# A message-passing layer: vector operations over messages cut to 128 columns and spread over the units

## The chip, the cores and the metric

The kernel runs on one core of a Trainium2 chip. The core has a matrix engine (TensorE, PE in the profile; PEld is its weight load), a vector engine (VectorE, DVE), an engine for activations (ScalarE, ACT), GpSimd (POOL), which here issues the indirect gathers, and SyncE (SP), which issues the other DMAs. The metric is the device time of one execution in microseconds; the median of three runs counts.

## The reference

There are 6250 nodes with 256 features and 206250 edges, sorted by their target `dst`. Cut to what matters:

```python
h = relu(layernorm(x))
polarity = clip(edge_attr[:, 0:1], 0, 1)
e = relu(edge_attr[:, 1:] @ W_e1.T + b_e1) @ W_e2.T + b_e2      # 64 -> 256 -> 256
edge_emb = (e * (polarity + 0.01)) @ W_le.T + b_le
msg = relu(h[src] + edge_emb)
aggr = segment_sum(msg, dst, num_segments=6250)
g = layernorm((h + aggr) @ W_g1.T + b_g1) * ln_g + ln_b
out = x + relu(g) @ W_g2.T + b_g2
```

All of it is in float32.

## The kernel before, in words

The two products W_e2 and W_le are multiplied once into one matrix (`wc_s`), and the polarity is a number per edge, so that it can be multiplied in at the end. Edges lie in tiles of 128. A block is four tiles (512 edges), a unit is half a block (two tiles, 256 edges; there are 806 units, numbered `u`), a pair is two blocks, and a group is six blocks (24 tiles, 3072 edges; 68 groups). Nodes are worked on in 49 windows of 128.

First the statistics of the rows of x are made and h + b_le is written to a table in HBM (`hb_d`, L370, L372). Meanwhile the edge work of the first 22 units begins. The main loop (L710) then runs over the units. For each unit:

- `forward(u)` computes the edge part: eight matrix instructions on PE (L266; every listed matmul is two of them in the profile) fill one PSUM tile, and one DVE add (L271) takes it to `msg[u]` in SBUF. There are seven such PSUM tiles in rotation (`pz`); the first layer, the edge part and the node work all draw on them.
- Once every eight units (in the middle of the run, `by_two`), right behind one unit's edge part, `turn_of` runs the first layer of two pairs (L243, 16 matrix instructions that need eight PSUM tiles, six taken away by ACT at L251 and two by DVE at L248), then `add_pairs`, which sums finished messages into the groups with one-hot matrices (L566), and then loads the raw edge data ahead. I call the eight units from one such place to the next a round.
- `gathers(...)` puts the gathers of later units on the POOL queue (L528): two indirect DMAs per unit, 128 rows of the table each, into one of 16 buffers `hg`. The first gather of such a call also waits for the last matmul of the unit's edge part.
- `whole(made)` makes the message: per tile one DVE operation hg = msg x polarity + hg over 256 columns (L551), both large operands and the output in SBUF, the polarity a column of one number per partition; then one RELU on ACT for the unit (L556). It runs behind the edge part by `LEAD - u // 36` units, 22 at first and 1 at last, so that messages and gathers go a little faster than units.
- `due()` runs at most one step that has fallen due. The steps are the one-hot matrices of a later group (`select`, L541: one DVE comparison over 24 x 32 = 768 columns) and the node work of a window: `spread` loads x, its transpose `hT` and the row statistics `stb` and makes the window's one-hot matrices (L629); `ready(0)` and `ready(1)` (L639) multiply and add the statistics to `hT` over 256 columns; `offset` (L205) adds a bias to x; `rows_of`, `one`, `two` and `three` are the matrix steps.

The order on each engine is the order of the calls (a manual schedule): DVE works its list strictly in that order, and so does POOL. So what stands behind a waiting instruction on DVE waits with it. The calls in the loop, cut:

```python
for u in range(LEAD, NU):
    now = u
    forward(u)
    ...
        gathers(4 * summed + HG - 8 + (1, 2, 3, 4, 5, 6, 6, 7)[k], last_z)
    ...
    while made < u + 1 - max(LEAST, LEAD - u // SHRINK) - (by_two(u // 4) and (u + 1) % 8 == TURN):
        whole(made)
        made += 1
    due()
```

Of the kernel before, what the change touches and what calls it, by code (L numbers as in the profile page):

```python
# [51 lines left out]
def group_of(b):  # L52
    return b // L


def blocks_of(g):
    return range(g * L, min((g + 1) * L, NB))
# [36 lines left out]
def gnn_kernel(ctx: ExitStack, tc: tile.TileContext, x, src_c, dst_c, dst_r, pol_c, raw_t, w_e1t, w_e2,  # L94
# [16 lines left out]

    ident = const.tile([P, P], F32, name="ident")
    eps_t = const.tile([P, 1], F32, name="eps_t")
    we1_s = const.tile([P, D], F32, name="we1_s")
    wc_s = const.tile([P, 2, D], F32, name="wc_s")
    bc_s = const.tile([P, 2, D], F32, name="bc_s")
# [27 lines left out]
    def finish_nodes(nd, ps, w, n):  # L144

        r = w * P

        def turn(a):
            pt = ps()
            for c in range(2):  # L150
                nc.tensor.transpose(pt[:, 0, c * P:c * P + n], a[:n, c * P:(c + 1) * P], ident[:n, :n])
            aT = nd.tile([P, 2, P], F32, name="aT")
            if n == P:
                nc.scalar.activation(aT, pt[:, 0, :].rearrange("p (c n) -> p c n", c=2), AF.Copy)
            else:
                for c in range(2):
                    nc.scalar.activation(aT[:, c, :n], pt[:, 0, c * P:c * P + n], AF.Copy)
            return aT

        def first(aT, bias_by_pe=False):  # L160
            ph = ps()
            if bias_by_pe:
                nc.tensor.matmul(ph[:n, 0, :], ones[0:1, :n], bg1_b[0:1], start=True, stop=False)
            for c in range(2):
                nc.tensor.matmul(ph[:n, 0, :], aT[:, c, :n], wg1_s[:, c, :], start=c == 0 and not bias_by_pe, stop=c == 1)  # L165
            hs = nd.tile([P, D], F32, name="hs")
            if bias_by_pe:
                hb = ph[:, 0, :]
            else:
                hb = hs  # L170
                nc.vector.tensor_add(hs[:n], ph[:n, 0, :], bg1_b[:n])
            mv = row_stats(nd, n, 1, lambda i: hb[:n])
            rs = nd.tile([P, 1], F32, name="rs1")
            one_over_std(rs[:n], mv, n)
            nc.vector.tensor_scalar(hs[:n], hb[:n], mv[:n, 0, 0:1], rs[:n], op0=ALU.subtract, op1=ALU.mult)
            return hs

        def second(hs):
            pt = ps()
            for c in range(2):  # L180
                nc.tensor.transpose(pt[:, 0, c * P:c * P + n], hs[:n, c * P:(c + 1) * P], ident[:n, :n])  # L181
            nT = nd.tile([P, 2, P], F32, name="nT")
            for c in range(2):
                nc.scalar.activation(nT[:, c, :n], pt[:, 0, c * P:c * P + n], AF.Relu, bias=lnb_s[:, c:c + 1],  # L184
                                     scale=lng_s[:, c:c + 1])
            return nT

        def third(nT, xt):
            po = ps()
            for c in range(2):  # L190
                nc.tensor.matmul(po[:n, 0, :], nT[:, c, :n], wg2_s[:, c, :], start=c == 0, stop=c == 1)  # L191
            ot = nd.tile([P, D], F32, name="ot")
            nc.vector.tensor_add(ot[:n], po[:n, 0, :], xt[:n])
            for i, (a, b) in enumerate(spread_out(n)):
                eng = nc.scalar if i else nc.sync
                eng.dma_start(out=out[bass.ds(r + a, b - a), :], in_=ot[a:b])

        def load_x():
            xt = nd.tile([P, D], F32, name="xt3")
            for a, b in spread_out(n):  # L200
                nc.sync.dma_start(out=xt[a:b], in_=x[bass.ds(r + a, b - a), :])
            return xt

        def offset(xt):
            nc.vector.tensor_add(xt[:n], xt[:n], bg2_b[:n])  # L205

        return turn, first, second, third, load_x, offset

# [3 lines left out]
    with fast:  # L212
# [11 lines left out]
        def ps():  # L224
            return psz.tile([P, 2, D], F32, name="pz")
# [74 lines left out]
                turn_of(u // 4)  # L300

        nc.vector.memset(eps_t, EPS)
        nc.vector.memset(ones, 1.0)
        nc.vector.memset(rs_s, 0.0)
        nc.vector.memset(nm_s, 0.0)
# [207 lines left out]
        with tc.tile_pool(name="hg", bufs=HG) as hg_p, tc.tile_pool(name="ms", bufs=5) as ms_p, \  # L513
# [21 lines left out]

            def select(g):

                n = len(blocks_of(g)) * S
                t = g * L * S
                sel[g] = sel_p.tile([P, L * S, W], F32, name="sel")  # L540
                nc.vector.tensor_tensor(  # L541
                    sel[g][:, :n, :], iota_w.rearrange("p (o w) -> p o w", o=1).to_broadcast([P, n, W]),
                    rel[:, t:t + n].rearrange("p (t o) -> p t o", o=1).to_broadcast([P, n, W]), ALU.is_equal)

            def whole(u):

                m = msg.pop(u)
                if plain(u):
                    nc.vector.tensor_add(m, m, bc_s)
                for i in range(2):  # L550
                    nc.vector.scalar_tensor_tensor(hg[u][:, i, :], m[:, i, :], pol_s[:, 2 * u + i:2 * u + i + 1],  # L551
                                                   hg[u][:, i, :], op0=ALU.mult, op1=ALU.add)
                    if u == NU - 1:
                        nc.scalar.activation(hg[u][:, i, :], hg[u][:, i, :], AF.Relu)
                if u < NU - 1:
                    nc.scalar.activation(hg[u], hg[u], AF.Relu)  # L556

            def add_up(b):

                g = group_of(b)  # L560
                k = b - g * L
                if k == 0:
                    acc[g] = pd[:, g % 2, :] if g < NG - 1 else ps()[:, 0, :]
                for j in range(S):
                    m = hg[2 * b + j // 2]
                    nc.tensor.matmul(acc[g][j * W:(j + 1) * W, :], sel[g][:, k * S + j, :], m[:, j % 2, :],  # L566
                                     start=k == 0, stop=b == blocks_of(g)[-1])
                hg.pop(2 * b)
                hg.pop(2 * b + 1)
                return g if b == blocks_of(g)[-1] else None  # L570
# [16 lines left out]
            def add_pairs(last=False):  # L587

                nonlocal summed
                whole_groups = []  # L590
                while summed < NP and min(4 * summed + 4, NU) < made + last:
                    for b in (2 * summed, 2 * summed + 1):
                        if b < NB:
                            whole_groups.append(add_up(b))
                            if b % L == 0 and group_of(b) + 2 < NG:
                                at(now + 2, lambda g=group_of(b) + 2: select(g))
                    summed += 1

                for g in whole_groups:
                    keep(g)  # L600
# [2 lines left out]
            todo = {}  # L603
            now = 0
            late = {}
            ending = {-2: [], -1: []}

            def at(u, fn):
# [2 lines left out]
            def node_work(w, spread_now=False):  # L611
# [7 lines left out]
                def spread():  # L619
# [7 lines left out]
                    for g in gs:  # L627
# [1 line left out]
                        nc.vector.tensor_scalar(s2, iota_p, rowid[:, g:g + 1], float(-w * P), op0=ALU.subtract,  # L629
                                                op1=ALU.is_equal)  # L630
                        box["sel2"].append(s2)
                    at(now + 3, lambda: ready(0))
                    at(now + 4, lambda: ready(1))
                    at(now + 5, lambda: offset(box["xt"]))

                def ready(i):

                    hT, st = box["hT"], box["st"]
                    nc.vector.tensor_tensor(hT[:, :, :n], hT[:, :, :n], st[:, i:i + 1, :n].to_broadcast([P, 2, n]),  # L639
                                            (ALU.mult, ALU.add)[i])  # L640

                def sums_of(part):

# [56 lines left out]

            gathers(HG)
            sums = add_pairs
            for i, fn in ((0, first_rows), (1, rows_of_edges), (3, lambda: select(0)), (5, row_numbers), (6, stats_out),
                          (7, lambda: select(1)), (8, node_weights)):
                at(LEAD + i, fn)
            for i, fn in enumerate((by_group(0, ALU.max), by_group(1, ALU.min), by_row(0, ALU.max), by_row(1, ALU.min),
                                    verdict, count, total)):
# [2 lines left out]
            for u in range(LEAD, NU):  # L710
# [8 lines left out]
                else:  # L719
                    gathers(4 * summed + HG - 4 + (u - TURN) % 4 + 1, last_z)  # L720

                while made < u + 1 - max(LEAST, LEAD - u // SHRINK) - (by_two(u // 4) and (u + 1) % 8 == TURN):
                    whole(made)
                    made += 1
                due()
                if u == NU - 24:
                    for w in range(NW):
                        if groups_of(w)[-1] == NG - 1:
                            late[w] = node_work(w, True)
                if u == LEAD + 60:  # L730
                    flag = nc.values_load(bad_i[0:1, 0:1], min_val=0, max_val=3 * P)
            while todo:
                now = min(todo)
                for fn in todo.pop(now):
                    fn()
            before, last = ending[-2], ending[-1]
            for sums_of, halves_out, rows_of, one, two, three, gs in before:
                rows_of()
# [28 lines left out]
def any_order(tc, dram, v):  # L767
# [7 lines left out]
    with tc.tile_pool(name="sc", bufs=1) as sc, tc.tile_pool(name="sk", bufs=2) as sk, \  # L775
# [78 lines left out]
        def nodes(w, n):  # L854
# [1 line left out]
            nc.sync.dma_start(out=ac[:n], in_=acc_d[bass.ds(w * P, n), :])  # L856
            turn, one, two, three, load_x, offset = v["finish_nodes"](sk, lambda: sp1.tile([P, 1, D], F32, name="ps_a"), w, n)
            xt = load_x()
            offset(xt)
            three(two(one(turn(ac))), xt)  # L860

        with tc.For_i(0, full, 1) as w:
# [65 lines left out]
```

## Time and profile before

| what | value |
|---|---|
| median of the runs | 2187.48 us (2186.34 to 2188.13, three runs) |
| the profiled execution | 2189.23 us, its span 2187.4 us |
| mean granted TensorE clock | 0.997 |
| PE, PEld busy | 2169.5, 1625.1 us |
| DVE busy | 1604.4 us |
| ACT busy | 960.8 us |
| POOL busy | 1648.4 us |
| DMA | 309.17 MB, mean 141 GB/s |

A row of the page's table of groups names the line, the engine, the operation, what it writes and reads, its shape and count; then the busy time in us and the mean duration of one in ns; then the idle time of that engine just before such instructions, and what ended most of it. Busy times count overlapping instructions once, and an instruction may start before the one ahead of it on its engine has ended, so a mean duration is longer than the distance between two starts. In a list of waits the columns are the waiting group, what it waited for, the total in us, the number of times and the longest. A timeline line gives start and length in us; several instructions of one kind in a row are merged, with their number behind x.

### The profile page before, as it was taken

How to read it: one execution, taken by the hardware profiler on the slowest of the kernel's cores; microseconds unless marked ns; L12 is line 12 of the kernel's file. 1: busy time of each engine (PE TensorE's matmuls, PEld its weight loads, DVE VectorE, ACT ScalarE, POOL GpSimd, SP SyncE). 2: the span in 40 equal slices, each digit the busy share in tenths (PEclk: the TensorE clock that was granted, in tenths of full speed). 3: DMA queues.
4: the chain of work that ended last, by engine and by line, in shares of the span. 5: the costliest groups of instructions: out<-in, count | busy, mean ns of one | idle time of the engine just before them, and what ended most of it. 6: DMA issues, size and time to landing. Idle time of an engine off the chain costs nothing.

```text
span 2187.4 us, 34907 instructions
## 1 busy us (share of the span) xinstructions
PE 2169.5 (99%) x12382; PEld 1625.1 (74%) x12382; DVE 1604.4 (73%) x3470; ACT 960.8 (44%) x1701; POOL 1648.4 (75%) x1675
## 2 busy tenths in 40 slices
PE   9999999999999999999999999999999999999998
PEld 6677777777777777777677777777777777777776
DVE  7787777777777777777677777777777767777675
ACT  7444444444444444444444444343444444444443
POOL 5777777777777777777777777777777777777775
PEclk9999999999999999999999999999999999999999
DMA  9544445454545454545544445445444445454543
GB/s 313 159 134 134 138 126 157 130 149 122 151 126 155 119 155 125 151 123 151 142 122 139 142 139 151 129 121 156 139 131 128 143 130 153 131 146 130 150 123 89
DMA packets 156075, 309.17 MB, mean 141 GB/s; under 512 B 33183, under 2 KB 77944, under 8 KB 155896
## 3 DMA queue, kind: packets, MB, share of 16 engines
q0 software_dynamic: 77376, 211.39, 33.7%
q1 hardware_dynamic: 77364, 92.23, 13.7%
q10 hardware_dynamic: 1156, 3.28, 0.4%
q8 instruction: 98, 1.61, 0.3%
q14 instruction: 81, 0.66, 0.1%
HBM read 293.92 MB, written 12.85 MB: 140 GB/s over the span
## 4 chain that ended last, share of the span: by engine, by line
PE 92%; DMA 3%; POOL 2%; DVE 2%; issue 1%; ACT 1%; ACTq 0%; DVEq 0%; POOLq 0%
PE pz L266 60%; PE pz L243 16%; PE pd L566 9%; PE pz L664 3%; DMA hg<-hb_d,src_s 3%; PE pz L165 2%; PE pz L191 2%; POOL hg L528 2%; DVE msg L271 1%; PE pz L181 1%; DMA xt<-in_x_dram 0%; ACT xt L366 0%; DVE hg L551 0%; DVE st L136 0%; PE pz L307 0%
## 5 line engine op out<-in xcount | busy, mean ns | idle before, releaser
L528 POOL DMA_INDIRECT hg<-hb_d,src_s x1612 | 1611.2, 999 | 495.5 <-issue 355.3
L266 PE MATMUL pz<-wc_s,e 128*128 128x256 f32 x6448 | 1452.3, 381 | 1.3 <-ACT msg L269 1.3
L266 PEld LDWEIGHTS pz<-wc_s,e 128*128 128x128 f32 x6448 | 1208.7, 190 | 203.8 <-issue 28.8
L556 ACT ACTIVATE hg<-hg 128x512 f32<-128x512 f32 x805 | 500.5, 629 | 1048.0 <-DVE hg L551 1030.5
L551 DVE SCALAR_TENSOR_TENSOR hg<-msg,pol_s,hg 128x256 f32<-128x256 f32 x1612 | 711.3, 478 | 153.3 <-DMA hg<-hb_d,src_s 148.9
L271 DVE TENSOR_TENSOR msg<-pz,bc_s 128x512 f32<-128x512 f32 x799 | 542.9, 685 | 224.0 <-PE pz L266 223.0
L243 PE MATMUL pz<-raw,we_s 64*128 64x512 f32 x1612 | 402.8, 608 | 6.9 <-DVE msg L271 6.6
L251 ACT ACTIVATE e<-pz,vecs 128x512 f32<-128x512 f32 x605 | 361.8, 692 | 88.0 <-PE pz L243 86.9
L243 PEld LDWEIGHTS pz<-raw,we_s 64*128 64x128 f32 x1612 | 160.2, 186 | 195.6 <-issue 127.2
L248 DVE TENSOR_SCALAR e<-pz,vecs 128x512 f32<-128x512 f32 x201 | 150.5, 749 | 164.6 <-PE pz L243 164.6
L566 PE MATMUL pd<-hg,sel 128*32 128x256 f32 x3216 | 196.9, 386 | 0.0
L566 PEld LDWEIGHTS pd<-hg,sel 128*32 128x32 f32 x3216 | 95.0, 110 | 129.3 <-issue 77.6
L664 PEld LDWEIGHTS pz<-s,ms 128*128 128x128 f32 x548 | 68.7, 192 | 3.1 <-issue 0.4
L664 PE MATMUL pz<-s,ms 128*128 128x128 f32 x548 | 69.3, 275 | 0.1
L541 DVE TENSOR_TENSOR sel<-iota_w,rel 128x768 f32<-128x768 f32 x68 | 63.9, 940 | 0.0
L370 POOL TENSOR_TENSOR hb<-xt,rows_b 128x256 f32<-128x256 f32 (+1 forms) x49 | 34.1, 728 | 24.2 <-ACT xt L366 18.2
L191 PE MATMUL pz<-wg_s,nT 128*128 128x256 f32 (+1 forms) x196 | 50.6, 380 | 0.6 <-ACT nT L184 0.6
L165 PE MATMUL pz<-wg_s,hT 128*128 128x256 f32 (+1 forms) x196 | 50.5, 380 | 0.0
L577 ACT ACTIVATE ms<-pd 128x256 f32<-128x256 f32 x66 | 25.4, 384 | 51.5 <-PE pd L566 51.5
L191 PEld LDWEIGHTS pz<-wg_s,nT 128*128 128x128 f32 (+1 forms) x196 | 37.1, 190 | 5.9 <-ACT nT L184 0.8
L165 PEld LDWEIGHTS pz<-wg_s,hT 128*128 128x128 f32 (+1 forms) x196 | 37.0, 190 | 5.7 <-issue 0.3
L639 DVE TENSOR_TENSOR hT<-hT,stb 128x256 f32<-128x256 f32 x98 | 40.8, 417 | 0.0
(90 smaller groups left out, 378.2 us busy)
## 6 DMA issues: line engine op xcount, KB each, us to landing
raw<-in_raw_t_dram SPq DMA_DIRECT2D x202, 256.0 KB
hg<-hb_d,src_s POOLq DMA_INDIRECT x1612
stb<-st_d SPq DMA_DIRECT2D x49, 128.0 KB
hb_d<-hb SPq DMA_DIRECT2D x12, 512.0 KB
xt<-in_x_dram SPq DMA_DIRECT2D x48, 128.0 KB
hT<-in_x_t_dram SPq DMA_DIRECT2D x48, 128.0 KB
out_dram<-ot SPq DMA_DIRECT2D x48, 128.0 KB
xt<-in_x_dram SPq DMA_DIRECT2D x11, 512.0 KB
```

Of the source, the lines that this page charges most:

```text
L165: nc.tensor.matmul(ph[:n, 0, :], aT[:, c, :n], wg1_s[:, c, :], start=c == 0 and not bias_by_pe, stop=c == 1)
L191: nc.tensor.matmul(po[:n, 0, :], nT[:, c, :n], wg2_s[:, c, :], start=c == 0, stop=c == 1)
L243: nc.tensor.matmul(pe[s, c], we1_s[s * F:(s + 1) * F, c * P:(c + 1) * P], raw[q][s * F:(s + 1) * F, :], start=True, stop=True)
L248: nc.vector.tensor_scalar(e1[b][:, c, :], pe[s, c], be1_s[:, c:c + 1], 0.0, op0=ALU.add, op1=ALU.max)
L251: nc.scalar.activation(e1[b][:, c, :], pe[s, c], AF.Relu, bias=be1_s[:, c:c + 1])
L266: last_z = nc.tensor.matmul(pz[:, i, :], e1[b][:, c, k:k + P], wc_s[:, c, :], start=c == 0, stop=c == 1)
L271: nc.vector.tensor_add(msg[u], pz, bc_s)
L528: g = nc.gpsimd.indirect_dma_start(out=hg[u][:, i, :], out_offset=None, in_=hb_d, in_offset=bass.IndirectOffsetOnAxis(ap=src_s[:, 2 * u + ...
L551: nc.vector.scalar_tensor_tensor(hg[u][:, i, :], m[:, i, :], pol_s[:, 2 * u + i:2 * u + i + 1], hg[u][:, i, :], op0=ALU.mult, op1=ALU.add)
L556: nc.scalar.activation(hg[u], hg[u], AF.Relu)
L566: nc.tensor.matmul(acc[g][j * W:(j + 1) * W, :], sel[g][:, k * S + j, :], m[:, j % 2, :], start=k == 0, stop=b == blocks_of(g)[-1])
L664: nc.tensor.matmul(pa[:, c, :n], ms[g][:, c * P:(c + 1) * P], box["sel2"][i][:, :n], start=i == 0, stop=i == len(gs) - 1)
```

## The change

The products of `whole` become two operations of 128 columns each in place of one of 256. The one-hot of a group is no longer one comparison of 768 columns but six of 128, one per block; `ready` works on one half of `hT` at a time and `offset` on one half of x. These pieces also change their form: a two-operand TENSOR_TENSOR becomes a SCALAR_TENSOR_TENSOR that first adds a column of zeros (`zero_c`), so that the values stay the same. They leave the list of due steps and go into two queues, `steps` (h and x; due three units after the loads) and `rest` (one-hot). `piece()` runs one of them per unit, between the edge part's add and the products; where more than six one-hot pieces wait, a second runs after `due()`. The first sums of a group first run what is left of its one-hot.

```diff
+    zero_c = const.tile([P, 1], F32, name="zero_c")
...
-        def offset(xt):
-            nc.vector.tensor_add(xt[:n], xt[:n], bg2_b[:n])
+        def offset(xt, c):
+            h = slice(c * P, (c + 1) * P)
+            nc.vector.scalar_tensor_tensor(xt[:n, h], xt[:n, h], zero_c[:n], bg2_b[:n, h], op0=ALU.add, op1=ALU.add)
...
             def select(g):
-                n = len(blocks_of(g)) * S
-                t = g * L * S
-                sel[g] = sel_p.tile([P, L * S, W], F32, name="sel")
-                nc.vector.tensor_tensor(
-                    sel[g][:, :n, :], iota_w.rearrange("p (o w) -> p o w", o=1).to_broadcast([P, n, W]),
-                    rel[:, t:t + n].rearrange("p (t o) -> p t o", o=1).to_broadcast([P, n, W]), ALU.is_equal)
+                return [(g, lambda k=k: rows_of_block(g, k)) for k in range(len(blocks_of(g)))]
+
+            def rows_of_block(g, k):
+                t = (g * L + k) * S
+                if k == 0:
+                    sel[g] = sel_p.tile([P, L * S, W], F32, name="sel")
+                nc.vector.scalar_tensor_tensor(
+                    sel[g][:, k * S:(k + 1) * S, :], iota_w.rearrange("p (o w) -> p o w", o=1).to_broadcast([P, S, W]),
+                    zero_c, rel[:, t:t + S].rearrange("p (t o) -> p t o", o=1).to_broadcast([P, S, W]), op0=ALU.add,
+                    op1=ALU.is_equal)
+
+            def piece():
+                if steps and steps[0][0] <= now:
+                    steps.popleft()[1]()
+                elif rest:
+                    rest.popleft()[1]()
...
                 for i in range(2):
-                    nc.vector.scalar_tensor_tensor(hg[u][:, i, :], m[:, i, :], pol_s[:, 2 * u + i:2 * u + i + 1],
-                                                   hg[u][:, i, :], op0=ALU.mult, op1=ALU.add)
+                    for c in range(2):
+                        h = slice(c * P, (c + 1) * P)
+                        nc.vector.scalar_tensor_tensor(hg[u][:, i, h], m[:, i, h], pol_s[:, 2 * u + i:2 * u + i + 1],
+                                                       hg[u][:, i, h], op0=ALU.mult, op1=ALU.add)
...
                 if k == 0:
                     acc[g] = pd[:, g % 2, :] if g < NG - 1 else ps()[:, 0, :]
+                    while rest and rest[0][0] <= g:
+                        rest.popleft()[1]()
...
                             if b % L == 0 and group_of(b) + 2 < NG:
-                                at(now + 2, lambda g=group_of(b) + 2: select(g))
+                                rest.extend(select(group_of(b) + 2))
...
-                    at(now + 3, lambda: ready(0))
-                    at(now + 4, lambda: ready(1))
-                    at(now + 5, lambda: offset(box["xt"]))
+                    steps.extend((now + 3, lambda i=i, c=c: ready(i, c)) for i in range(2) for c in range(2))
+                    steps.extend((now + 3, lambda c=c: offset(box["xt"], c)) for c in range(2))
-                def ready(i):
+                def ready(i, c):
                     hT, st = box["hT"], box["st"]
-                    nc.vector.tensor_tensor(hT[:, :, :n], hT[:, :, :n], st[:, i:i + 1, :n].to_broadcast([P, 2, n]),
-                                            (ALU.mult, ALU.add)[i])
+                    nc.vector.scalar_tensor_tensor(hT[:, c, :n], hT[:, c, :n], zero_c, st[:, i, :n], op0=ALU.add,
+                                                   op1=(ALU.mult, ALU.add)[i])
...
-            for i, fn in (..., (3, lambda: select(0)), ..., (7, lambda: select(1)), (8, node_weights)):
+            for i, fn in (..., (3, lambda: rest.extend(select(0) + select(1))), ..., (8, node_weights)):
...
                 else:
                     gathers(4 * summed + HG - 4 + (u - TURN) % 4 + 1, last_z)
 
+                piece()
                 while made < ...:
                     whole(made)
                     made += 1
                 due()
+                if len(rest) > 6:
+                    piece()
...
+            while steps:
+                steps.popleft()[1]()
```

More of the change, by code (lines that the diff above doesn't have):

```diff
@@ L302, in gnn_kernel @@
         nc.vector.memset(eps_t, EPS)
+        nc.vector.memset(zero_c, 0.0)
         nc.vector.memset(ones, 1.0)
@@ L605, in gnn_kernel @@
             late = {}
+            steps = deque()
+            rest = deque()
             ending = {-2: [], -1: []}
@@ L702, in gnn_kernel @@
             sums = add_pairs
-            for i, fn in ((0, first_rows), (1, rows_of_edges), (3, lambda: select(0)), (5, row_numbers), (6, stats_out),
-                          (7, lambda: select(1)), (8, node_weights)):
+            for i, fn in ((0, first_rows), (1, rows_of_edges), (3, lambda: rest.extend(select(0) + select(1))), (5, row_numbers), (6, stats_out),
+                          (8, node_weights)):
                 at(LEAD + i, fn)
@@ L858, in nodes @@
             xt = load_x()
-            offset(xt)
+            offset(xt, 0)
+            offset(xt, 1)
             three(two(one(turn(ac))), xt)
```

## The prediction

> **What bounds the kernel now.** I read the page's first part and its groups first, for who is busy and with what.
>
> ```profile
> PE 2169.5 (99%) x12382; PEld 1625.1 (74%) x12382; DVE 1604.4 (73%) x3470; ACT 960.8 (44%) x1701; POOL 1648.4 (75%) x1675
> ...
> L528 POOL DMA_INDIRECT hg<-hb_d,src_s x1612 | 1611.2, 999 | 495.5 <-issue 355.3
> ...
> L551 DVE SCALAR_TENSOR_TENSOR hg<-msg,pol_s,hg 128x256 f32<-128x256 f32 x1612 | 711.3, 478 | 153.3 <-DMA hg<-hb_d,src_s 148.9
> L271 DVE TENSOR_TENSOR msg<-pz,bc_s 128x512 f32<-128x512 f32 x799 | 542.9, 685 | 224.0 <-PE pz L266 223.0
> L243 PE MATMUL pz<-raw,we_s 64*128 64x512 f32 x1612 | 402.8, 608 | 6.9 <-DVE msg L271 6.6
> ```
>
> PE is at 99%, but POOL has no free moment either: the first gather starts at 64.5 us, the last ends at 2168.9 us, and of these 2104 us 1611 are gathers and about 492 the fixed 0.305 us between two (1612 of them). In the list of waits, POOL's own are all at that 0.3 us, whatever name stands on the right, so nobody holds it up for long:
>
> ```profile
> POOL hg L528 <- PE pz L266: 39.6, 130, 0.3
> POOL hg L528 <- ACT hg L556: 26.5, 87, 0.3
> ...
> DVE hg L551 <- DMA hg<-hb_d,src_s: 148.9, 199, 2.8
> PEld pz L243 <- DVE msg L271: 41.1, 81, 3.1
> ```
>
> The last two lines are one chain: a gather is late, the product at L551 waits, the add at L271 behind it in DVE's order is late, its PSUM tile is not free, and the first layer on PE (L243, eight PSUM tiles in a row) stands. The timeline shows it whole:
>
> ```profile
> 1082.08 0.48 DVE L551 SCALAR_TENSOR_TENSOR hg<-msg,pol_s,hg 128x256 f32<-128x256 f32 x1 [1.77 <-DMA hg<-hb_d,src_s]
> ...
> 1082.48 1.28 DVE L271 TENSOR_TENSOR msg<-pz,bc_s 128x512 f32<-128x512 f32 x2
> ...
> 1083.22 2.04 PE L243 MATMUL pz<-raw,we_s 64*128 64x512 f32 x6 [1.55 <-DVE msg L271]
> ```
>
> PE's timeline gives what that costs: a block of 16 such matmuls takes 3.63 us to the next line when nothing is late, more when something is.
>
> ```profile
> 1014.55 4.83 PE L243 MATMUL pz<-raw,we_s 64*128 64x512 f32 x16
> ...
> 1036.53 3.70 PE L243 MATMUL pz<-raw,we_s 64*128 64x512 f32 x16
> 1040.16 1.93 PE L566 MATMUL pd<-hg,sel 128*32 128x256 f32 x32
> ```
>
> 95 blocks at 3.63 and 11.5 half-size ones at 1.92 make 367 us; the page has 402.8. So some 36 us of stall (with L566's share 37), of which 6 fall at 91 us, when the gather buffers fill for the first time, and 1.5 in one L566 block that waits for nobody. About 29 us are stalls for late gathers. All other PE segments sit at their floor, so PE's own limit is a span of 2187.4 - 29 = 2158 us.
>
> Why a gather is long: the median is 0.947 us, the mean 0.999, and 85 us in all lie above the median. This is one:
>
> ```profile
> 1007.42 0.95 DVE L541 TENSOR_TENSOR sel<-iota_w,rel 128x768 f32<-128x768 f32 x1
> ...
> 1007.74 1.46 POOL L528 DMA_INDIRECT hg<-hb_d,src_s  x1 [0.30 <-PE pz L266]
> 1008.29 0.68 DVE L271 TENSOR_TENSOR msg<-pz,bc_s 128x512 f32<-128x512 f32 x1
> ...
> 1008.89 0.87 DVE L551 SCALAR_TENSOR_TENSOR hg<-msg,pol_s,hg 128x256 f32<-128x256 f32 x2
> ```
>
> The one-hot runs to 1008.37, the gather ends at 1009.20, 0.83 later. Counted over the trace, a gather that, 0.13 us after its start, meets a DVE operation with both inputs in SBUF always ends 0.82 us after that operation's end. Sorted by the operation waited for: L551 37 us (281 gathers, 0.33 at most), L541 26, L639 11, L205 8, others 3. Behind an L551 the three TENSOR_TENSORs sometimes carry the wait across two operations (1.0 us at most); L551 behind L551 never does.
>
> **The change part by part.** *DVE time.* No row is a 128-column product. Starts of neighbours give the pitch: L541 to L271 above is 0.87 us for 768 columns; L639 (256) is followed after 0.335; slope 0.267 per 256 columns, 0.068 fixed. L551 pairs have 0.87 - 0.48 = 0.393, so 0.126 fixed with a column as scalar. At 128 columns: 0.133 + 0.126 = 0.26 us. [...] Products: 3224 x 0.26 - 1612 x 0.393 = +204 us. Pieces: 403 of the one-hot, 196 of h, 98 of x, 697 x 0.26 = 181, in place of 67 x 0.869 + 98 x 0.335 + 49 x 0.335 = 107: +74. DVE goes from 1604 to 1882 us, 87% of the span.
>
> What hides it is DVE's waiting for PE: 223 us before L271 and 165 before L248, 388 in all. Round by round (8 units), with these pitches on the order of the built program: from the first add after L566 to the last before L243, DVE has 13.5 us of work on average (11.4 now) against 13.9 of PE at its floor. PE first needs the last add's tile 2.7 us into L243's block, and the add takes 0.69, so DVE may be 2.0 us late; in 6 of 94 rounds the work exceeds PE's time by over 1 us, in two by over 2. Between L248 and the next add stand 2.4 us (1.6 now) against 2.9. So cost on the path: nothing, with 0.4 us a round to spare where there were 2.5. If that cover is gone, each microsecond is PE's.
>
> *Gathers.* An operation holds a gather up from about 0.11 us after its start: 0.37 of L551's 0.48, 0.235 of a half's 0.345. Random meetings weigh as count x hold squared / 2: 1612 x 0.137 / 2 = 110 becomes 3224 x 0.055 / 2 = 89, so 37 us become 30. The 697 pieces weigh 19, so 6. The 45 us of the three TENSOR_TENSORs go. Rest 3: about 40 in place of 85. Bounds: none left, or the unopened chain below. POOL then needs 64.5 + 1612 x 1.253 + 40 + 2 + the tail of 18.5 (2187.4 - 2168.9) = 2145 us, 13 less than PE's 2158. The bound passes from POOL to PE.
>
> *Order.* Pieces stand between the add and the products of the unit, so the products, the RELU and the next add queue behind each, 0.26 us. The first piece of h waits for two loads issued three units (over 5 us) before, as it did. No DMA is added or moved on a queue; the gathers keep their place and their waits. PE keeps its matmuls, node steps moving by a unit where the list of due steps is shorter.
>
> *Sum.* Of the 29 us, gathers a mere 0.6% faster than PE will not save all: they gain on PE only slowly, so early rounds still wait. I keep a quarter: 29 - 7 = 22. Span 2187.4 - 22 = 2165; the profiled execution was 2189.2, 1.8 above its span and 1.7 above the median 2187.5, so the median is to be about 2165.
>
> **The rivals.**
> *Spare time lost (2187).* Gathers get shorter, but DVE with 0.4 us a round to spare no longer absorbs a wait of 0.75 us (148.9 / 199), so fewer waits each cost more: 29 us stay. For: 2.1 us more work a round. Against: 388 us of PE waits, and waits should become rare. Equally 2187 if the halves chain as the TENSOR_TENSORs did.
>
> *DVE becomes the bound (slower).* Place: the last add before L243; it decides once DVE is over 2.0 us late there. At a pitch of 0.30, 32 operations add 1.3 us a round, lateness 0.8 on average; a third of the rounds (my estimate from the spread above) would pass 2.0 by some 0.7 us: +22, and with the gather stalls kept about 2209. [...] For: L551's durations overlap now by only 0.085. [...]
>
> *The lock never opens (slower, 2260).* If four halves in a row leave a gather no opening, it waits for the rest of the chain: 1.04 us held, 0.52 on average, against 0.79 and 0.17. 37 x (1.04 x 0.52) / (0.79 x 0.17) = 149, and 149 + 6 + 3 - 85 = +73 us on a POOL that never rests: 2260. For: the TENSOR_TENSORs do this. Against: L551 behind L551 never did in 281 cases. [...]
>
> **How the numbers follow.** Forecast 0.55, at 2155 to 2178; spare time lost 0.18 (0.13 within 0.2%, 0.05 a little faster); DVE bound 0.17; lock 0.10. 0.2%, 4.4 us, is about what a measurement of this kernel tells from no change. Faster 0.60, same 0.13, slower 0.27. Range: 2150 (all 37 us of stall gone) to 2210 (DVE at a pitch of 0.30); beyond lie the lock and the upper end of the pitch, under 0.2.
>
> **What would show it.** Mean of the gathers near 0.973 and none over 1.3 us; POOL with waits longer than 0.3; L243 near 382 us; DVE at 1880; halves 0.26 apart. L243 over 400 with DVE lines ahead of it would show lateness; gathers of 1.5 us and more the lock.

## The result, and the profile after

The changed kernel takes 2241.47 us (median of five runs, 2234.55 to 2246.48), the kernel before 2187.48 us: a ratio of 1.0243, interval [1.0221, 1.0264]. It is slower, by 54 us, where 22 us less were forecast. The profiled execution is the lowest of the five, 2234.55 us with a span of 2232.7, so what follows explains 45 us of span (2187.4 before). The granted clock was 0.993 in place of 0.997, but the matmuls of the edge part (L268) are busy for 1452.4 us, as before (1452.3), so the clock is not the cause.

The page's first part and its groups, in the columns described above; the lines have moved (L528 is L531 now, L551 L568, L541 L548, L271 L273, L243 L245):

```profile
PE 2203.7 (99%) x12382; PEld 1633.6 (73%) x12382; DVE 1870.8 (84%) x5565; ACT 963.5 (43%) x1701; POOL 1686.0 (76%) x1675
...
L531 POOL DMA_INDIRECT hg<-hb_d,src_s x1612 | 1648.8, 1023 | 504.4 <-issue 369.5
...
L568 DVE SCALAR_TENSOR_TENSOR hg<-msg,pol_s,hg 128x128 f32<-128x128 f32 x3224 | 911.6, 343 | 85.3 <-DMA hg<-hb_d,src_s 83.8
L273 DVE TENSOR_TENSOR msg<-pz,bc_s 128x512 f32<-128x512 f32 x799 | 543.5, 682 | 101.9 <-PE pz L268 100.4
L245 PE MATMUL pz<-raw,we_s 64*128 64x512 f32 x1612 | 432.9, 619 | 18.0 <-DVE msg L273 17.4
```

DVE is where it was forecast (1870.8 us against 1882), and the halves start 0.26 us apart. But the gathers have a mean of 1.023 us, not 0.973, and the first layer has become longer (402.8 to 432.9 us), not shorter. The list of waits says the same from the other side:

```profile
DVE msg L273 <- PE pz L268: 100.4, 156, 3.0
DVE hg L568 <- DMA hg<-hb_d,src_s: 83.8, 108, 2.3
PEld pz L245 <- DVE msg L273: 76.3, 115, 3.3
```

DVE has lost over half of its spare time (223 us of waiting for the edge part before, 100 now), it waits less often for a gather, and PE stands longer for DVE: 41 us before, 76 now.

POOL still has no rest, so its path can be summed. The first gather starts at 64.4 us; 1612 gathers at the median and 1612 fixed pauses, 1612 x (0.947 + 0.305), are 2018.2; the gathers' time above the median is 123.1, pauses longer than 0.305 add 11.5, and 17.2 lie behind the last gather. That is 2234 us, for a span of 2232.7. The same sum for the kernel before is 64.5 + 2018.2 + 85.2 + 2.5 + 18.5 = 2189 for 2187.4. The terms cover the whole span, so they must add up; what says that POOL is the bound is that its pauses exceed the fixed 0.305 by only 11.5 us in all. So the 45 us are 38 of longer gathers and 9 of longer pauses, less 1 at the end.

What makes a gather longer is seen in the timeline of the changed kernel, 180 us from its start (all engines; the lines of other engines are left out):

```profile
179.25 0.34 DVE L548 SCALAR_TENSOR_TENSOR sel<-iota_w,zero_c,rel 128x128 f32<-128x128 f32 x1
179.51 1.13 DVE L568 SCALAR_TENSOR_TENSOR hg<-msg,pol_s,hg 128x128 f32<-128x128 f32 x4
179.85 1.60 POOL L531 DMA_INDIRECT hg<-hb_d,src_s  x1 [0.30 <-PE pz L268]
180.56 0.68 DVE L273 TENSOR_TENSOR msg<-pz,bc_s 128x512 f32<-128x512 f32 x1
...
181.42 1.13 DVE L568 SCALAR_TENSOR_TENSOR hg<-msg,pol_s,hg 128x128 f32<-128x128 f32 x4
...
181.76 1.61 POOL L531 DMA_INDIRECT hg<-hb_d,src_s  x1 [0.30 <-issue]
```

The four halves of a unit run from 179.51 to 180.64. The gather starts at 179.85 and meets the second half; it is let in neither at that half's end nor at the third's, but at the fourth's, and ends at 181.45, 0.81 us behind 180.64. The next one does the same, 0.65 us over the median like the first. Before, no gather waited through two products. Now, counted over the trace, 441 gathers wait through one operation (48 us), 62 through two (25 us), 65 through three (42 us) and 4 through four (4 us). Of those caught in a second half, 101 are let in at its end and 60 only behind the fourth; of 77 caught in a first half, only 4 wait on.

### The profile page after: what moved, and what is told of

It reads as the page before. It is cut to its first block, busy times and chain, and to the rows that moved or that the text cites. A ratio compares the mean times of both kernels' runs of the same rounds, so it can differ in the third digit from the quotient of the medians.

```text
span 2232.7 us, 37809 instructions
## 1 busy us (share of the span) xinstructions
PE 2203.7 (99%) x12382; PEld 1633.6 (73%) x12382; DVE 1870.8 (84%) x5565; ACT 963.5 (43%) x1701; POOL 1686.0 (76%) x1675
## 5 line engine op out<-in xcount | busy, mean ns | idle before, releaser
L531 POOL DMA_INDIRECT hg<-hb_d,src_s x1612 | 1648.8, 1023 | 504.4 <-issue 369.5
L268 PE MATMUL pz<-wc_s,e 128*128 128x256 f32 x6448 | 1452.4, 381 | 1.0 <-ACT msg L271 1.0
L268 PEld LDWEIGHTS pz<-wc_s,e 128*128 128x128 f32 x6448 | 1209.3, 190 | 203.7 <-issue 23.0
L573 ACT ACTIVATE hg<-hg 128x512 f32<-128x512 f32 x805 | 505.8, 629 | 1124.4 <-DVE hg L568 1027.1
L568 DVE SCALAR_TENSOR_TENSOR hg<-msg,pol_s,hg 128x128 f32<-128x128 f32 x3224 | 911.6, 343 | 85.3 <-DMA hg<-hb_d,src_s 83.8
L273 DVE TENSOR_TENSOR msg<-pz,bc_s 128x512 f32<-128x512 f32 x799 | 543.5, 682 | 101.9 <-PE pz L268 100.4
L245 PE MATMUL pz<-raw,we_s 64*128 64x512 f32 x1612 | 432.9, 619 | 18.0 <-DVE msg L273 17.4
L245 PEld LDWEIGHTS pz<-raw,we_s 64*128 64x128 f32 x1612 | 167.2, 188 | 226.7 <-issue 106.6
L548 DVE SCALAR_TENSOR_TENSOR sel<-iota_w,zero_c,rel 128x128 f32<-128x128 f32 x403 | 137.2, 341 | 3.2 <-PE pd L585 3.2
L659 DVE SCALAR_TENSOR_TENSOR hT<-hT,zero_c,stb 128x128 f32<-128x128 f32 (+1 forms) x196 | 66.9, 341 | 0.0
```

Source lines behind the costliest of these rows:

```text
L245: nc.tensor.matmul(pe[s, c], we1_s[s * F:(s + 1) * F, c * P:(c + 1) * P], raw[q][s * F:(s + 1) * F, :], start=True, stop=True)
L268: last_z = nc.tensor.matmul(pz[:, i, :], e1[b][:, c, k:k + P], wc_s[:, c, :], start=c == 0, stop=c == 1)
L273: nc.vector.tensor_add(msg[u], pz, bc_s)
L531: g = nc.gpsimd.indirect_dma_start(out=hg[u][:, i, :], out_offset=None, in_=hb_d, in_offset=bass.IndirectOffsetOnAxis(ap=src_s[:, 2 * u + ...
L548: nc.vector.scalar_tensor_tensor(sel[g][:, k * S:(k + 1) * S, :], iota_w.rearrange("p (o w) -> p o w", o=1).to_broadcast([P, S, W]), zero_ ...
L568: nc.vector.scalar_tensor_tensor(hg[u][:, i, h], m[:, i, h], pol_s[:, 2 * u + i:2 * u + i + 1], hg[u][:, i, h], op0=ALU.mult, op1=ALU.add)
```

## The experiments

Two theories were put up. Theory G: the loss is POOL's, by gathers that wait through chains of halves. Theory D: the loss is DVE's, which comes late to the PSUM tiles of the first layer. The runs used four chips. On three of them the kernel before takes 2587 to 2600 us, on the fourth 2188 (there ran g5 and h1 to h3); each run is compared with the kernel before on its own chip. Times are medians; "extra" is the gathers' time above 0.947 us, counted over the trace.

| run | this, us | before, us | ratio, interval | extra, us |
|---|---|---|---|---|
| e1 pieces only | 2613.56 | 2593.28 | 1.0085 [1.0056, 1.0114] | 71 |
| e2 halves only | 2619.01 | 2593.28 | 1.0109 [1.0074, 1.0145] | 165 |
| e3 load only | 2605.16 | 2593.28 | 1.0059 [1.0036, 1.0082] | 107 |
| e4 spacer | 2662.19 | 2593.28 | 1.0287 [1.0250, 1.0323] | 48 |
| f1 pieces only | 2619.15 | 2592.28 | 1.0113 [1.0057, 1.0168] | 64 |
| f2 halves only | 2616.96 | 2592.28 | 1.0107 [1.0050, 1.0165] | 175 |
| f3 load only | 2603.77 | 2592.28 | 1.0045 [1.0024, 1.0067] | 108 |
| f4 spacer | 2663.86 | 2592.28 | 1.0254 [1.0194, 1.0315] | 50 |
| g1 changed | 2635.15 | 2597.52 | 1.0154 [1.0104, 1.0204] | 166 |
| g2 before | 2600.04 (one time) | 2597.52 | | 114 |
| g3 changed, half POOL | 2187.78 | 2597.52 | 0.8428 [0.8393, 0.8464] | |
| g4 before, half POOL | 2157.00 | 2597.52 | 0.8309 [0.8274, 0.8344] | |
| g5 form only | 2176.79 | 2188.02 | 0.9945 [0.9927, 0.9964] | 67 |
| h1 pieces, half POOL | 2153.31 | 2188.02 | 0.9838 [0.9819, 0.9856] | |
| h2 halves, half POOL | 2165.25 | 2188.02 | 0.9892 [0.9874, 0.9911] | |
| h3 load, half POOL | 2156.80 | 2188.02 | 0.9853 [0.9835, 0.9872] | |
| i1 pieces, all gathers | 2614.18 | 2587.21 | 1.0112 [1.0065, 1.0160] | 70 |
| i2 halves, all gathers | 2615.23 | 2587.21 | 1.0113 [1.0068, 1.0158] | 164 |

### The parts alone, a load without reads, and a spacer (e1 to e4)

The expected times of e1 to e4 and f1 to f4 are for a chip on which the kernel before takes 2187 us, so that only what they say of the gathers can be compared. e1 is the changed kernel with its products uncut:

```diff
-                    for c in range(2):
-                        h = slice(c * P, (c + 1) * P)
-                        nc.vector.scalar_tensor_tensor(hg[u][:, i, h], m[:, i, h], pol_s[:, 2 * u + i:2 * u + i + 1],
-                                                       hg[u][:, i, h], op0=ALU.mult, op1=ALU.add)
+                    nc.vector.scalar_tensor_tensor(hg[u][:, i, :], m[:, i, :], pol_s[:, 2 * u + i:2 * u + i + 1],
+                                                   hg[u][:, i, :], op0=ALU.mult, op1=ALU.add)
```

> Theory G (gathers): the loss is gathers held up by the four half products in a row, which often give no opening between them; the pieces themselves help. Then with products of 256 columns again and the pieces kept, the gathers' time above their median falls from 123 us (changed kernel) and 85 us (before) to 45 to 60 us, and the time is 2165 to 2175 us, faster than before. Theory D (DVE load): the loss is DVE's own lateness. Then DVE at about 1680 us busy (before 1604, changed 1871) gives a quarter of the loss, 2195 to 2205 us, whatever the gathers do.

e2 is the kernel before with the same lines the other way round: only the products are cut.

> G: halves' 100 us and the 45 us or more of the one-hot, h and x operations behind them add up: 140 to 180 us above the gathers' median, time 2245 to 2275 us. D: DVE about 1800 us busy, three quarters of the loss, 2220 to 2230 us.

e3 is the kernel before with DVE work that reads nothing from SBUF, behind each product:

```diff
+                    nc.vector.memset(spare[:, :P], 0.0)
```

> The kernel before with DVE time added that reads nothing: a memset of 128 columns (0.127 us by the start distance of such a memset before) behind each product, 0.25 us a unit, the same added DVE time as the halves bring. G: the gathers stay near 85 us above their median, 2187 to 2200 us. D: 2220 to 2235 us.

e4 is the changed kernel with an operation of one column between the halves of the unit's two tiles:

```diff
+                    if i == 0:
+                        nc.vector.memset(spare[:, 0:1], 0.0)
```

> The changed kernel with a memset of one column between the two tiles' products of a unit, so that at most two half products stand next to each other. G: the carrying over three operations ends, gathers 60 to 85 us above their median, 2180 to 2205 us although DVE has 45 us more to do. D: DVE at about 1915 us, 2245 to 2260 us.

On the gathers the four speak clearly. Cutting the products alone lengthens them (165 us extra; the kernel before has 114 on such a chip, g2). Cutting the pieces alone shortens them (71). DVE work that reads nothing from SBUF does not lengthen them (107). One column of memset in the middle of the four halves takes the changed kernel from 166 (g1) to 48, with only two halves left in a row in the program's order: gathers that wait through more than one operation go from 215 to 1. So the carrying needs the unbroken row of halves. Theory G had expected 45 to 60 us extra in e1, 140 to 180 in e2, near 85 in e3 and 60 to 85 in e4; only e2 lies inside, and e4 went further than expected. (The memset leaves no gap in time: in e4's trace it starts a median of 0.02 us after the third half, and the two halves around it start 0.27 us apart.) On the time they don't decide: e4, with the shortest gathers, is the slowest. On these chips POOL pauses between gathers for hundreds of us beyond the fixed 0.305 (866 us in g2's row below, of which 1612 x 0.305 are 492), so the length of the gathers alone does not set the time there. Why e4 is the slowest was not found: its DVE is busy for 1867.6 us, 5 more than the changed kernel's in g1.

### The same four again (f1 to f4)

> The kernel of e1 again, since on the first chip every kernel, the one before among them, took 2580 to 2670 us and all engines often stood for nothing the profile shows, so POOL did not bound anything there. There the gathers stood 71 us above their median (85 before, 123 changed). Theory G (gathers): 60 to 75 us above the median and 2170 to 2182 us on a chip where the kernel before takes 2187. Theory D (DVE load): 2195 to 2205 us.

> The kernel of e2 again. On the first chip 165 us above the gathers' median. G: the same here, and since POOL bounds the kernel, 2187 + 80 = 2260 to 2275 us, slower than the changed kernel although DVE does less. D: 2220 to 2230 us.

> The kernel of e3 again (DVE time added that reads nothing). On the first chip 107 us above the gathers' median. G: 2187 + 22 = about 2205 us, of which none is DVE's lateness. D: 2220 to 2235 us.

> The kernel of e4 again. On the first chip 48 us above the gathers' median, the lowest of all, though DVE has the most to do. G: POOL gets 37 us less to do than before, 2155 to 2175 us unless something else stops it. D: 2245 to 2260 us. A time near 2200 with short gathers would say that both count.

All four came out as before, to within 0.4%. The order of the times (load, then pieces and halves alike, then the spacer) is not the order of the gathers' extra time.

### Both kernels on such a chip (g1, g2)

> The changed kernel itself on the chip of these runs, where the kernel before takes 2592 us and POOL stands 320 to 500 us between gathers in all kernels so far, so that POOL's rate can't be the bound. Theory G (the loss is POOL's longer gathers alone): within 0.5% of the kernel before, 2580 to 2605 us, while the gathers stand some 100 us or more above their median. Theory D (DVE late, PE stands in the first layer): 2% or more slower here too, 2640 to 2660 us.

> The kernel before with a trace on this chip. Both theories: about 2592 us; the gathers some 85 us above their median as on the first chip, or more if the good phase of products and gathers there was luck (a random meeting would give L551 alone about 70 to 84 us). It shows where all engines lose 400 us here.

The change costs 1.5% there, which lies between the two theories (0.5% and 2%). The gathers' extra time rises by 52 us (114 to 166), the time by 38. The page's POOL group of the kernel before on this chip shows what is different:

```profile
L528 POOL DMA_INDIRECT hg<-hb_d,src_s x1612 | 1639.1, 1017 | 865.9 <-issue 584.6
```

The gathers themselves are little longer (1.017 us against 0.999), but POOL idles 866 us in front of them instead of 496, most of it waiting for nothing that the profile shows.

### Half of the gathers taken off POOL (g3, g4)

To see the kernels without POOL's bound, the second gather of each unit becomes a plain load of the same size on SP. It loads other rows than the gather, so the output of these kernels is not the reference's:

```diff
-                    for i in range(2):
+                    nc.sync.dma_start(out=hg[u][:, 1, :], in_=hb_d[(u % 48) * P:(u % 48 + 1) * P, :])
+                    for i in range(1):
                         g = nc.gpsimd.indirect_dma_start(
```

> The changed kernel with the second gather of each unit replaced by a plain load of 128 table rows on SP's queue (wrong rows, as many bytes), so POOL has half its work. To be read against the next run. D: slower than it by 2% or more. G: the same as it within 0.5%.

> The kernel before with the same replacement: POOL at half its work. G, on a chip where POOL bounds: 20 to 30 us faster than before (PE's floor); here, where POOL doesn't bound: within 1% of before. D: the same.

g4 takes 2157.0 us, span 2155.4: near the 2158 that the prediction gave as PE's own limit. Neither theory expected this on such a chip (within 1% of the 2598 before): all of the extra 400 us are gone. g3 takes 2187.8: without POOL's bound the change still costs 31 us, 1.4%, more than theory G's 0.5% and less than theory D's 2%. Theory G alone falls. Counted by line over PE's instructions, 28.9 of them lie in the first layer (373.0 us in g4's blocks, 402.0 in g3's); no other group moves by over 1 us. One block late, in the timeline of g3 (first the lines of DVE, then those of PE):

```profile
1163.79 0.42 DVE L172 TENSOR_TENSOR hs<-pz,rows_b 128x256 f32<-128x256 f32 x1
...
1165.45 0.41 DVE L176 TENSOR_SCALAR hs<-hs,mv,rs 128x256 f32<-128x256 f32 x1
1165.78 0.68 DVE L273 TENSOR_TENSOR msg<-pz,bc_s 128x512 f32<-128x512 f32 x1
1166.38 0.34 DVE L660 SCALAR_TENSOR_TENSOR hT<-hT,zero_c,stb 128x128 f32<-128x128 f32 x1
1166.64 1.13 DVE L569 SCALAR_TENSOR_TENSOR hg<-msg,pol_s,hg 128x128 f32<-128x128 f32 x4
1167.69 0.68 DVE L273 TENSOR_TENSOR msg<-pz,bc_s 128x512 f32<-128x512 f32 x1
1168.29 0.34 DVE L660 SCALAR_TENSOR_TENSOR hT<-hT,zero_c,stb 128x128 f32<-128x128 f32 x1
1168.55 1.13 DVE L569 SCALAR_TENSOR_TENSOR hg<-msg,pol_s,hg 128x128 f32<-128x128 f32 x4
1169.60 0.68 DVE L273 TENSOR_TENSOR msg<-pz,bc_s 128x512 f32<-128x512 f32 x1
```

```profile
1166.86 2.85 PE L245 MATMUL pz<-raw,we_s 64*128 64x512 f32 x12
1170.34 1.81 PE L245 MATMUL pz<-raw,we_s 64*128 64x512 f32 x4 [0.64 <-DVE msg L273]
1172.08 0.64 PE L586 MATMUL pd<-hg,sel 128*32 128x256 f32 x8
```

No gather is waited for here. A node step (L172 to L176, two us with its reply from ACT) stands on DVE just ahead of the block; from then on DVE works add, piece, four halves, add, piece, four halves, add, at 1.91 us a unit without a gap. The third of these adds ends at 1170.28, and 0.06 later PE goes on: the block takes 5.22 us in place of 3.63.

### Which part makes the 31 us (h1, h2, h3)

The kernels of e1, e2 and e3 with half of the gathers replaced in the same way:

> The changed kernel with products of 256 columns again (so the pieces of the one-hot, of h and of x, with their place ahead of the products and the node steps moved by it), and the second gather of each unit replaced by a plain load of 128 table rows, so that its output is not the reference's. The two kernels in this form stood at 2157.0 (before) and 2187.8 us (changed): 31 us that gathers cannot explain. Theory H (the halves' DVE time of some 200 us makes DVE late): the pieces add only 75 us of DVE, so 2157 to 2164. Theory P (the pieces' place: 0.26 us ahead of each unit's products, and node steps that now fall due just ahead of the first layer's PE block): 2175 to 2188. If each gives its part in proportion to its DVE time: 2165.

> The kernel before with the products in halves alone, and the second gather of each unit replaced in the same way (output not the reference's). Theory H: 2175 to 2188. Theory P: 2157 to 2164. In proportion to DVE time: 2180. The gathers should still be carried through the chains of halves by either theory: over 1.3 us some of them, without effect on the time, as POOL now rests half of the time.

> The kernel before with a memset of 128 columns behind each product, and the second gather of each unit replaced in the same way (output not the reference's). The memsets add some 90 us to DVE's busy time (1587 to 1675 with all gathers) and nothing that reads SBUF. If DVE's time alone makes the loss: 31 x 90 / 270 = 10, so about 2167; if lateness has a threshold (spare time of 2.5 us in each eight units, of which this takes 0.9): 2157 to 2160.

Neither part makes it. The pieces alone are 4 us faster than g4 (theory P falls), the halves alone 8 us slower (less than theory H asked), both together 31. It does not go in proportion to DVE's time either, since h3, with 85 us more of it, stands at 2156.8. The rows point to the spare time that is left. These are the waits of DVE for the edge part and those of the first layer for DVE, in g4 (before), h1 (pieces), h2 (halves) and g3 (both):

```profile
DVE msg L271 <- PE pz L266: 270.8, 279, 6.2
...
PEld pz L243 <- DVE msg L271: 8.9, 31, 0.3
```

```profile
DVE msg L273 <- PE pz L268: 233.5, 294, 3.5
...
PEld pz L245 <- DVE msg L273: 8.4, 34, 0.3
```

```profile
DVE msg L271 <- PE pz L266: 142.5, 213, 2.8
...
PEld pz L243 <- DVE msg L271: 21.1, 57, 1.4
```

```profile
DVE msg L273 <- PE pz L268: 109.0, 169, 5.6
...
PEld pz L245 <- DVE msg L273: 29.1, 54, 2.4
```

From 271 down to 234 us of spare time nothing is lost, and no wait of PE in these rows is over 0.3 us; in h3, with 220 us, the longest is 0.5 and nothing is lost either; at 143 the longest is 1.4, at 109 it is 2.4. Of the 95 blocks of 16 matmuls, so many are over 0.5 us late: 3 in g4, none in h1, 5 in h3, 12 in h2, 17 in g3. g4 and g3 ran on a chip of the slower kind, h1 to h3 on the fourth; that they may be compared is assumed, not shown (g4 did not run on the fourth chip).

### The form without the cuts (g5)

The kernel before with the three TENSOR_TENSORs uncut and in their place, only written in the changed form, here the one-hot:

```diff
-                nc.vector.tensor_tensor(
+                nc.vector.scalar_tensor_tensor(
...
-                    rel[:, t:t + n].rearrange("p (t o) -> p t o", o=1).to_broadcast([P, n, W]), ALU.is_equal)
+                    zero_c, rel[:, t:t + n].rearrange("p (t o) -> p t o", o=1).to_broadcast([P, n, W]), op0=ALU.add,
+                    op1=ALU.is_equal)
```

> The kernel before, with the one-hot, the steps of h and the bias of x uncut and in their place, each written as a SCALAR_TENSOR_TENSOR with a column of zeros in place of a TENSOR_TENSOR; all gathers. If it is the form that carries a gather's wait on to the next operation, the 45 us of the gathers that waited behind these three shrink to the single operations' own holds (a one-hot of 768 columns still holds up to 0.9 us): 25 to 35 us. If it is any two operations in a row that leave no opening, they stay at about 45. The time: no more than 0.5% from the kernel before by either, as DVE's time is the same within 10 us.

```profile
PE 2158.7 (99%) x12382; PEld 1619.7 (74%) x12382; DVE 1613.2 (74%) x3471; ACT 960.9 (44%) x1701; POOL 1631.1 (75%) x1675
...
L530 POOL DMA_INDIRECT hg<-hb_d,src_s x1612 | 1593.8, 989 | 498.6 <-issue 353.9
...
L554 DVE SCALAR_TENSOR_TENSOR hg<-msg,pol_s,hg 128x256 f32<-128x256 f32 x1612 | 705.4, 478 | 96.1 <-DMA hg<-hb_d,src_s 93.4
```

This one is faster than the kernel before, by 0.55%, just over the 0.5% of the expectation. The gathers behind the three operations cost 17 us in place of 45 (one-hot 13.5, h 1.6, x 1.5), less than the expectation gave, and waiting through two operations falls from 45 gathers and 26 us to one gather and 0.7 us. The form was the carrier. POOL's sum is 63.8 + 2018.2 + 66.6 + 5.6 + 20.3 = 2174.5, for a span of 2174.4, and its pauses exceed the fixed ones by only 5.6 us: POOL is still the bound. Of the 18.6 us taken from the gathers 13 came off the span; 5 went into longer pauses and the tail. DVE is busy for 9 us more.

### The parts alone with all gathers (i1, i2)

These were to show the parts where POOL is the bound.

> The changed kernel with products of 256 columns again, all gathers. POOL's path is 64 us to the first gather, 1612 x 1.253 us, some 4 us of longer gaps, 18 us behind the last gather, that is 2106 us plus the time of the gathers above their median; the kernel with half the gathers replaced shows 2153 us without POOL's bound. Theory G (with the halves gone, POOL sets the time): the gathers' extra time is 60 to 75 us, so 2166 to 2181, faster than the kernel before, and no halves, no loss. Theory P (the pieces' place costs time where POOL is full): over 2188.

> The kernel before with the products in halves alone, all gathers. Without POOL's bound this kernel shows 2165 us. Theory G (the halves carry waiting gathers over to the end of their chain, and POOL has no rest): 115 to 135 us above the median, so 2221 to 2241, nearly all of the change's loss, and gathers of over 1.3 us behind products by the dozen. Theory D (only DVE's lateness, 8 to 12 us from the halves): 2196 to 2200, with gathers near the 85 us of the kernel before.

They ran on a chip of the slower kind, where the kernel before takes 2587 us, so the expected times could not be tested; they repeat e1 and e2. That the halves alone would make most of the 38 us of longer gathers on the faster kind of chip is therefore inferred from the gathers (164 and 165 us extra in i2 and e2, 70 and 71 in i1 and e1), not shown by a time.

## Why the prediction was wrong

*What bounds the kernel now: right.* POOL has next to no pause beyond its fixed ones (2.5 us before, 11.5 changed, 5.6 in g5), and PE's own limit, 2158 us, was measured at 2155.4 with POOL relieved. It is no strict limit: h1 has a span of 2151.3.

*DVE time: right.* The pitch of a half is 0.26 us as worked out (one lasts 0.343, the author's upper end of the pitch), DVE's busy time 1871 us against 1882.

*"So cost on the path: nothing, with 0.4 us a round to spare": wrong.* It costs 31 us once POOL is out of the way (g3 against g4). The prediction counted the work of a round against PE's time for it and found six rounds in 94 over by 1 us, two by over 2, the tolerance. In g3, 15 of the 95 blocks of 16 matmuls are over 1 us late. The average of 0.4 us says little about a round whose node step falls just ahead of the block. With all gathers this loss does not add to POOL's: the longer of two paths counts, 2233 for POOL and 2184 for PE and DVE. What of it reaches the result are at most the 9 us by which POOL's pauses have grown, which could come from buffers handed back late; that was not separated, and for 13 of the 16 pauses over 0.33 us the trace shows nothing that was waited for. If g3's span of 2184 may be taken over to a kernel with all gathers, this step alone would have left 3 us of the 22 that were forecast (an estimate).

*"So 37 us become 30 … about 40 in place of 85": wrong, and this is the step that turned the sign.* The products' gathers cost 102 us, the pieces 16 (10, 4 and 2, where 6 were forecast). The working took halves to let a gather in as whole products did, because "L551 behind L551 never did in 281 cases". That was true of 256 columns and false of 128: 131 gathers wait through two operations or more. Nor is it the number in a row alone: in the kernel before, where two units are made at once, four products of 256 columns stand in a row, and all 65 gathers caught in one of the first three were let in at its end. The hold from about 0.11 us after an operation's start is near the traces: 0.13 us after the start of a gather that then waited, the half it met had run for at least 0.11 us in the changed kernel, the product for at least 0.15 in the kernel before. The part of the step that struck 45 us for the three TENSOR_TENSORs held, and g5 shows that the form alone saves 28 of them (of which the products' gathers, by meeting more, take back 8: 85 us extra become 67).

*The rivals.* "The lock never opens" named the mechanism, at 149 us for the products in place of the 102 measured: a gather caught in a second half is held to the end of the row in 60 of 161 cases, one caught in a first half in 4 of 77. It gave 2260 for 2241 us and had a chance of 0.10; the range ended at 2210. "DVE becomes the bound" had the right place, the last adds before the first layer, but by a longer pitch, which did not come.

*What was to show it* did show it: gathers of 1.5 us and more, and L245 over 400 us with DVE lines ahead of it.

## What to carry to other kernels

When one engine never rests and waits through another's operations, as POOL does here through DVE's, look at what these leave open between them, not only at how long each is: cutting a product in two made each operation shorter (0.48 to 0.34 us), and 131 gathers waited through two or more in a row. Try a change of form and a change of size apart; here the form alone was worth 0.5%, and with the new sizes and places the change lost 2.4%. And a mean of spare time per round covers added work only as far as the worst rounds have some too: the mean was worked out at 0.4 us here, and in g3 15 of 95 blocks were over 1 us late.

## What the hardware did that was not expected

Operations in an unbroken row, all with both large inputs in SBUF, differ in whether they let a waiting gather in between them. Products of 256 columns did (no gather of the kernel before waits through two of them, and in g5 one waited through two operations); two-operand TENSOR_TENSORs behind a product (45 gathers of the kernel before) and products of 128 columns (131 gathers of the changed kernel wait through two operations or more) often did not; and one column of memset between opened the row (166 us to 48). A gather that waits ends a median of 0.82 us behind the operation at which it is let in, in both kernels. The place in the row counts as well: in e2, in rows of four halves and nothing else, all 105 gathers caught in one of the first two were let in at its end, and 99 of 115 caught in the third were held through the fourth. Why size and place decide was not found.

The same program took 2188 us on one chip and 2587 to 2600 on three others. There PE, DVE and POOL all show slow stretches (in f3, from 1500 to 1504 us, PE is busy for 1.69 us and DVE not at all), with a mean granted clock of 0.935 to 0.951 in the traces in place of 0.997 (the kernel before); in the list of waits of the kernel before, POOL's wait for nothing shown has grown from 355 us with at most 0.9 at a time to this:

```profile
POOL hg L528 <- issue: 584.6, 1337, 6.0
```

With half of the gathers replaced by plain loads it is gone: g4 ran on such a chip, at 2157 us and a clock of 0.999. So the gathers on POOL have a part in it; what it is stays open.
